# A four-stage transformer block on one core: the two norm chains of a half interleaved, and the ends of the second attention rearranged

## The chip, the cores and the metric

The kernel runs on 1 core of one Trainium2 chip, all in fp32. The metric is the device time of one execution in microseconds (us). Before the change it was 1282.84, 1287.16 and 1286.2 us in three runs, a median of 1286.2 us.

A core has a matrix engine (TensorE, PE in the profile, with its weight loads shown apart as PEld), a vector engine (VectorE, DVE), an activation engine (ScalarE, ACT), a general engine (GpSimd, POOL) and a queue that issues transfers (SyncE, SP). Each works through its own instructions in order and waits for others by semaphores.

## The reference

The input is x, 1024 tokens of 256 channels. Four blocks follow each other, each added to x by the same rule:

```python
x = x + _layernorm(attn0(_layernorm(x)))   # softmax attention, 16 heads of 16, rope, own norm and residual inside
x = x + _layernorm(ffn0(_layernorm(x)))    # 8 experts of 256, all used, low-rank terms in two, routed weights
x = x + _layernorm(attn1(_layernorm(x)))   # 16 heads of 128: short convolution, silu, norm, then the recurrence
x = x + _layernorm(ffn1(_layernorm(x)))    # 16 experts of 176, top 4 of them weighted, and a shared one of 352
```

The recurrence of the second attention, for each head, is `S = (1 - b) * S + b * (v outer k)` and `o = S q`; o is multiplied by a silu gate and goes through Wo. Thus between any two blocks stand two layer norms: one of the block's output (added to x), and one of the new x (input of the next block).

## The kernel before

The kernel is written for a framework that allots tiles from pools and whose scheduler places each instruction in its engine's queue; calls marked to stay in program order keep their order. Tokens lie in 8 tiles of 128 (TT), worked in two halves of 512, a half in two pairs of tiles. Names that recur: `x` and `acc` hold the residual and the block's output by token; `hT` holds the normed x by channel, the input of the next block's matmuls.

*The two norms between blocks.* `turn_over` (L248) takes a pair when its `acc` is complete. For each tile DVE takes statistics (`st`, `mv`), forms `ve`; POOL raises it to −0.5 (`rs`); DVE forms `nb`, minus mean times rs. Then x becomes acc·rs + x (L257), the same statistics are taken of the new x, ACT writes h = x·rs2 + nb2 (L263), POOL adds the first norm's nb to x (L267), and PE transposes h (`turn`, L243), ACT copying to `hT` (L244). The mean of the first norm is left out of x at first, since the second norm takes it away; the POOL operation puts it in afterwards. The transposes are put on a list `todo`, which `catch_up` works off between later matmuls. `turn_over_slowly` (L194) is the same as a generator, advanced in steps beside the first attention; its lines are L201 to L236.

*First attention.* For two halves of queries and four groups of heads (8 steps), scores are computed twice: once to find each row's maximum (L517 and L448 scores, DVE reduces at L453), which goes into the query as an additional channel (`signed`, whose transposes are at L406 and copy at L407), and once transposed, exponentiated by ACT (L546, L535) and summed with the values by PE (L504). The two run interleaved; when no more maxima are left, the last group runs alone (`alone`). In the second half `finished_slowly` (L553) finishes the first half's tokens step by step; the second half's go on `todo` as `finished(1)`, with the product with `w_out` (L601) and its addition (L605).

*Experts.* A group of tiles of 128 hidden columns is worked by halves: `gates` calls `gated` (L757; pg, pu at L765, silu L767, product `mid` L768), then `catch_up`; `down` (L770 on; po L783, acc L791) projects back. `experts` (L795) orders them. In the last group's second half it runs two gate tiles, the previous half's down, the other tiles, and then the last down, calling `turn_over` for each pair.

*Second attention.* Heads run in pairs (groups g). `enter` makes keys and queries through `convolved` (px L1049, taps L1035 and L1041, silu L1059), beta through `shares` (pb L1007), decays (L1012), values and gates (L1183). `attend` does the recurrence in chunks of 128: transposed keys `ke` (L1225), scores `psc`/`pr` (L1231, L1233), states (L1239 to L1248), output `po` and `og` (L1257 to L1265). For the last head `output` projects head 14's and head 15's share by halves, so that `turn_over` can begin; at the end four of the norm chains run one after the other.

## Time and profile before

| what | us |
|---|---|
| median of three runs | 1286.2 |
| the profiled execution's time | 1286.36 |
| its span, first to last instruction | 1284.6 |
| PE busy | 1217.4 |
| DVE busy | 732.4 |
| ACT busy | 495.7 |
| POOL busy | 149.3 |
| mean granted clock of PE | 0.986 |

The first attention ends at about 304 us, the first experts at 488, the second attention at 1004, the second experts with the span. A row of the windows gives a stretch (from:to), its length, each engine's busy time with the number of its instructions, PE's granted clock (1.00 is full), the DMA share and GB/s. A row of the timeline gives the start, the length in us, the engine, the source line, what is written from what, how many instructions are taken together, and in brackets the engine's idle time before and what ended it.

### The profile page before, as it was taken

Reading aid. Unit: us, or ns where it says so; the run is one execution under the profiler, and the core shown is the slowest. Engines: PE = TensorE matmul, PEld = TensorE weight load, DVE = VectorE, ACT = ScalarE, POOL = GpSimd, SP = SyncE. Lnnn points to the kernel's source line nnn. Section 1 sums busy time; section 2 is a strip of 40 time slices with the busy share of each in tenths; the row PEclk is TensorE's granted clock in tenths of the full one; section 3 lists DMA queues with packets and bytes.
Section 4 is the critical chain, followed back from the end, with each engine's and each line's share of the span. In section 5 each row is a group of like instructions: output and inputs, shape, how many; then the busy total and the mean of one; then the engine's idle time right before and its main releaser. Section 6 shows DMA issues by size and latency. Waiting matters only on the chain. (4 is left out here: it accounts for less than half of the span.)

```text
span 1284.6 us, 15784 instructions
## 1 busy us (share of the span) xinstructions
PE 1217.4 (95%) x6128; PEld 722.3 (56%) x6128; DVE 732.4 (57%) x1656; ACT 495.7 (39%) x912; POOL 149.3 (12%) x137
## 2 busy tenths in 40 slices
PE   7999999989999997899999999999998799999997
PEld 4533333323556564567676667767676346555655
DVE  5876767641542345776777776758675523333334
ACT  4266665655411113544544454453543221111011
POOL 3100001010200022121111112121212400000001
PEclk9999999999999998999999999999999899999999
DMA  6000000000033012002021202020210105523000
GB/s 194 1 1 1 1 1 1 1 1 1 2 129 102 0 42 83 29 33 88 23 103 34 74 33 74 34 74 33 74 41 27 62 1 158 163 82 124 20 25 33
DMA packets 38923, 64.42 MB, mean 50 GB/s; under 512 B 4776, under 2 KB 28552, under 8 KB 38848
## 3 DMA queue, kind: packets, MB, share of 16 engines
q1 hardware_dynamic: 38848, 63.41, 15.4%
q8 instruction: 48, 0.79, 0.3%
q14 instruction: 27, 0.22, 0.1%
HBM read 62.12 MB, written 1.28 MB: 49 GB/s over the span
## 5 line engine op out<-in xcount | busy, mean ns | idle before, releaser
L453 DVE TENSOR_REDUCE pm<-sc 128x1 f32<-128x512 f32 x256 | 163.4, 685 | 66.1 <-PE sc L517 42.9
L768 DVE TENSOR_TENSOR mid<-sg,pu 128x512 f32<-128x512 f32 (+1 forms) x82 | 56.4, 688 | 192.7 <-PE pu L765 163.4
L517 PE MATMUL sc<-qTm,kT 32*128 32x512 f32 x512 | 152.5, 654 | 1.2 <-DVE pm L453 1.2
L767 ACT ACTIVATE sg<-pg 128x512 f32<-128x512 f32 (+1 forms) x82 | 48.9, 596 | 270.5 <-PE pg L765 270.4
L546 ACT ACTIVATE pe<-sc 128x512 f32<-128x512 f32 x216 | 117.8, 595 | 71.0 <-PE sc L517 48.8
L448 PE MATMUL sc<-kT,qT 32*128 32x512 f32 x512 | 139.1, 645 | 1.6 <-ACT qT L407 0.8
L1089 ACT ACTIVATE sn<-pt,shift,rs 128x128 f32<-128x128 f32 x256 | 93.6, 470 | 107.2 <-DVE shift L1085 107.0
L1049 PE MATMUL px<-hT,w_l1a 128*128 128x512 f32 x256 | 124.0, 596 | 4.3 <-issue 3.5
L1041 DVE SCALAR_TENSOR_TENSOR y<-px,cp,y 128x1023 f32<-128x1023 f32 (+5 forms) x102 | 123.2, 1211 | 2.5 <-ACT y L1035 2.5
L791 DVE TENSOR_TENSOR acc<-acc,po 128x512 f32<-128x512 f32 (+1 forms) x61 | 41.1, 674 | 100.1 <-PE po L783 100.1
L765 PE MATMUL pg<-hT,w_l1f 128*128 128x512 f32 (+1 forms) x200 | 97.1, 609 | 0.7 <-ACT hT L244 0.7
L765 PE MATMUL pu<-hT,w_l1f 128*128 128x512 f32 (+1 forms) x200 | 94.7, 596 | 0.0
L783 PE MATMUL po<-w_l1f,mid 128*128 128x256 f32 (+1 forms) x400 | 87.5, 379 | 0.0
L1084 POOL TENSOR_TENSOR rs<-ve,nhalf 128x8 f32<-128x8 f32 x32 | 52.4, 1638 | 299.8 <-DVE ve L1083 245.1
L504 PE MATMUL po<-pe,va 128*32 128x256 f32 (+1 forms) x872 | 80.9, 440 | 4.0 <-ACT oT L509 3.3
L783 PEld LDWEIGHTS po<-w_l1f,mid 128*128 128x128 f32 (+1 forms) x400 | 76.0, 190 | 13.4 <-issue 3.3
L517 PEld LDWEIGHTS sc<-qTm,kT 32*128 32x128 f32 x512 | 49.7, 187 | 53.7 <-issue 41.9
L184 POOL TENSOR_TENSOR rs<-ve,nhalf 128x2 f32<-128x2 f32 (+1 forms) x25 | 17.5, 701 | 464.2 <-DVE ve L183 459.7
L1183 PE MATMUL pg<-hT,w_l1a 128*128 128x512 f32 x128 | 61.9, 609 | 6.9 <-DVE og L1265 5.5
L504 PEld LDWEIGHTS po<-pe,va 128*32 128x32 f32 x872 | 17.8, 108 | 89.0 <-issue 77.5
L765 PEld LDWEIGHTS pu<-hT,w_l1f 128*128 128x128 f32 (+1 forms) x200 | 38.5, 192 | 49.5 <-issue 49.5
L765 PEld LDWEIGHTS pg<-hT,w_l1f 128*128 128x128 f32 (+1 forms) x200 | 38.1, 192 | 44.9 <-issue 43.5
(205 smaller groups left out, 1932.6 us busy)
## 6 DMA issues: line engine op xcount, KB each, us to landing
spread<-rows SPq DMA_DIRECT2D x32, 512.0 KB, 4.5
w<-w SPq DMA_DIRECT2D x16, 512.0 KB, 4.9
w_l1f<-in_e_gT SPq DMA_DIRECT2D x4, 640.0 KB, 4.0
w_l1f<-in_e_uT SPq DMA_DIRECT2D x4, 640.0 KB, 5.3
w_l1f<-in_e_dT SPq DMA_DIRECT2D x4, 640.0 KB, 8.0
w_l0f<-in_e_wg SPq DMA_DIRECT2D x4, 512.0 KB, 5.0
w_l0f<-in_e_wu SPq DMA_DIRECT2D x4, 512.0 KB, 6.5
w_l0f<-in_e_wd SPq DMA_DIRECT2D x4, 512.0 KB, 7.4
```

The source lines that it names most:

```text
L448: nc.tensor.matmul(sc, raw[r, tt * P : (tt + 1) * P], kT[r, g, half(kh)], start=True, stop=True,)
L453: nc.vector.tensor_reduce(pm[:, tt, 2 * pair + i, kh : kh + 1], sc, AX.X, ALU.max)
L504: nc.tensor.matmul(po[0][rows(j), c], va[:, st, g * G + j, :], pe[j // 2][:, j % 2, c], start=(st == 0), stop=(st == TT - 1 and c.stop == ...
L517: nc.tensor.matmul(sc, kT[rows(j), g, st * P : (st + 1) * P], qm[rows(j), :], start=True, stop=True,)
L546: nc.scalar.activation(pe[pair][:, i, :], sc, AF.Exp, scale=scale)
L765: nc.tensor.matmul(p, w(k), self.hT[:, k, c], start=(k == 0), stop=(k == KC - 1))
L768: nc.vector.tensor_tensor(mid, sg, pu, ALU.mult)
L783: nc.tensor.matmul(po[:, i, :], left[:, at * P : (at + 1) * P], right, start=(n == 0), stop=(n == len(pieces) - 1),)
L1041: nc.vector.scalar_tensor_tensor(y[:, at:hi], px[:, at - j : hi - j], column(cw + 4 * h + 3 - j), y[:, at:hi], ALU.mult, ALU.add,)
L1049: nc.tensor.matmul(px[:, c], w[:, k, hh * DK : (hh + 1) * DK], self.hT[:, k, c], start=(k == 0), stop=(k == KC - 1),)
L1089: nc.scalar.activation(sn[:, n, :], pts[n // 4][:, n % 4, :], AF.Identity, scale=rs[:, n : n + 1], bias=shift[:, n : n + 1],)
L1183: nc.tensor.matmul(pg, wg[:, k, hh * DK : (hh + 1) * DK], self.hT[:, k, c], start=(k == 0), stop=(k == KC - 1),)
```

## The change

- The two generators become one, `turning`, in 12 pieces, and its DVE instructions are pinned in program order. Means and rs of the first norm are kept for all three inner boundaries (`mvs`, `rss`); the first norm's `nb` and the shift of x on POOL at each boundary are gone. `nb` of the second norm is a piece of its own, after a yield.
- `turn_over` runs the first pair up to piece 5 and keeps it; with the second pair it goes on in turns: first to 10, second to 5, first to 12, second to 12.
- `shifted` adds the sum of the three kept shifts to x once, in the second experts at g == 3: four small POOL operations and eight on ACT.
- First attention: once the maxima are finished, `signed` is put off by two steps (`late`), and the finishing generator is advanced twice in each step.
- Experts: in the last group one gate tile, not two, comes ahead of the previous half's down. In the second experts the very first half's gates are done in two parts of 256 columns, with `catch_up(3)` between.
- Second attention, start: `decays` goes by halves, `begin` is cleared on POOL, and for head 0 decays(0), two calls of values and the first gate come before `catch_up`. End: for the last head `attend` is by_token(0), by_token(1), within(0), gathered(0), within(1), then the down of half 0 for both heads, gathered(1), and the half 1 products of both heads summed in two PSUM tiles (`sums`).
- The pools of all four stages get `reuse_waits="tile"`: a new tile waits for the tiles whose space it takes, not for a whole closed pool.

The diff, cut:

```diff
...
@@ -76,6 +76,9 @@
         self.nhalf = self.const.tile([P, TT], F32, name="nhalf")
         nc.gpsimd.memset(self.nhalf, -0.5)
         self.mv0 = self.const.tile([P, TT, 2], F32, name="mv0")
+        self.mvs = self.const.tile([P, 3, TT, 2], F32, name="mvs")
+        self.rss = self.const.tile([P, 3, TT], F32, name="rss")
+        self.norms = [0] * (TT // 2)
...
-        with tc.tile_pool(name="late", bufs=1) as late:
+        with tc.tile_pool(name="late", reuse_waits="tile", bufs=1) as late:
...
-        nc = self.nc
+    def pinned(self, ins):
+        return self.tc.keep_in_program_order(ins)
+    def turning(self, ps, tp, acc=None):
+        nc, pinned = self.nc, self.pinned
         xs, accs = self.pair(self.x, tp), self.pair(self.acc, tp)
         def small(tag, *shape):
@@ -198,41 +207,48 @@
         def stats(mv, i, src):
             st = self.small.tile([P, 6], F32, tag="st", name="st")
-            nc.vector.bn_stats(st, src)
-            nc.vector.bn_aggr(mv[:, i, :], st)
-        def scale(mv):
-            ve, rs, nb = small("ve"), small("rs"), small("nb")
-            nc.vector.tensor_scalar(ve, mv[:, :, 1], EPS, None, ALU.add)
+            pinned(nc.vector.bn_stats(st, src))
+            pinned(nc.vector.bn_aggr(mv[:, i, :], st))
+        def scale(mv, rs):
+            ve = small("ve")
+            pinned(nc.vector.tensor_scalar(ve, mv[:, :, 1], EPS, None, ALU.add))
             nc.gpsimd.tensor_tensor(rs, ve, self.nhalf[:, 0:2], ALU.pow)
-            nc.vector.scalar_tensor_tensor(nb, mv[:, :, 0], -1.0, rs, ALU.mult, ALU.mult)
-            return rs, nb
-        mv = small("mv", 2)
+        n = self.norms[tp]
+        self.norms[tp] += 1
+        mv, rs = (v[:, n, 2 * tp : 2 * tp + 2] for v in (self.mvs, self.rss))
         for i in range(2):
-            acc(i)
+            if acc is not None:
+                acc(i)
             yield
             stats(mv, i, accs[i])
             yield
-        rs, nb = scale(mv)
+        scale(mv, rs)
         yield
-        mv = small("mv", 2)
+        mv2, rs2 = small("mv", 2), small("rs")
         for i, x in enumerate(xs):
-            nc.vector.scalar_tensor_tensor(x, accs[i], rs[:, i : i + 1], x, ALU.mult, ALU.add)
+            pinned(nc.vector.scalar_tensor_tensor(x, accs[i], rs[:, i : i + 1], x, ALU.mult, ALU.add))
             yield
-            stats(mv, i, x)
+            stats(mv2, i, x)
             yield
-        rs2, nb2 = scale(mv)
+        scale(mv2, rs2)
+        yield
+        nb = small("nb")
+        pinned(nc.vector.scalar_tensor_tensor(nb, mv2[:, :, 0], -1.0, rs2, ALU.mult, ALU.mult))
+        yield
         h = self.row.tile([P, 2, D], F32, tag="h2", name="h")
         for i, x in enumerate(xs):
             nc.scalar.activation(
-                h[:, i, :], x, AF.Identity, scale=rs2[:, i : i + 1], bias=nb2[:, i : i + 1]
+                h[:, i, :], x, AF.Identity, scale=rs2[:, i : i + 1], bias=nb[:, i : i + 1]
             )
-            yield
-        for i, x in enumerate(xs):
-            nc.gpsimd.tensor_scalar(x, x, nb[:, i : i + 1], None, ALU.add)
+        ps = (yield) or ps
         self.turn(ps, h, tp)
         yield
+    SCALED, NORMED, PIECES = 5, 10, 12
...
-        xs = self.pair(self.x, tp)
-        rs, nb = self.scales(self.pair(self.acc, tp))
-        for i, x in enumerate(xs):
-            nc.vector.scalar_tensor_tensor(
-                x, self.acc[:, 2 * tp + i, :], rs[:, i : i + 1], x, ALU.mult, ALU.add
-            )
-        rs2, nb2 = self.scales(xs)
-        h = self.row.tile([P, 2, D], F32, tag="h2", name="h")
-        for i, x in enumerate(xs):
-            nc.scalar.activation(
-                h[:, i, :], x, AF.Identity, scale=rs2[:, i : i + 1], bias=nb2[:, i : i + 1]
-            )
-        for i, x in enumerate(xs):
-            nc.gpsimd.tensor_scalar(x, x, nb[:, i : i + 1], None, ALU.add)
-        self.todo.extend([None, None, lambda ps: self.turn(ps, h, tp)])
+        def take(t, n):
+            for _ in range(n):
+                next(t)
+        t = self.turning(ps, tts[0] // 2)
+        if tts[0] // 2 % 2 == 0:
+            take(t, self.SCALED)
+            self.first_pair = t
+            return
+        first = self.first_pair
+        take(first, self.NORMED - self.SCALED)
+        take(t, self.SCALED)
+        take(first, self.PIECES - self.NORMED)
+        take(t, self.PIECES - self.SCALED)
+        for t in (first, t):
+            self.todo.extend([None, None, lambda ps, t=t: t.send(ps)])
+    def shifted(self):
+        nc = self.nc
+        lost = self.small.tile([P, 3, TT], F32, tag="lost", bufs=1, name="lost")
+        shift = self.small.tile([P, TT], F32, tag="shift", bufs=1, name="shift")
+        nc.gpsimd.tensor_tensor(lost, self.mvs[:, :, :, 0], self.rss, ALU.mult)
+        nc.gpsimd.tensor_tensor(shift, lost[:, 0, :], lost[:, 1, :], ALU.add)
+        nc.gpsimd.tensor_tensor(shift, shift, lost[:, 2, :], ALU.add)
+        nc.gpsimd.tensor_scalar(shift, shift, -1.0, None, ALU.mult)
+        for tt in range(TT):
+            x = self.x[:, tt, :]
+            self.pinned(nc.scalar.activation(x, x, AF.Identity, bias=shift[:, tt : tt + 1]))
...
-            after = iter(())
+            after, then, late = iter(()), None, 2
             for n, (qh, g) in enumerate(steps):
                 if n == NG:
                     after = finished_slowly()
-                then = None
                 for inside in attend(qh, g, lambda: pulled == count):
                     if inside:
                         then = pull()
                         continue
-                    if then:
+                    if pulled == count and late > 0:
+                        late -= 1
+                    elif then:
                         then()
                         then = None
                     next(after, None)
+                    if pulled == count:
+                        next(after, None)
...
+    def gated(self, ps, tmp, wg, wu, mid, m, hf, part=None):
+        nc = self.nc
+        part = part or slice(0, HALF)
+        n = part.stop - part.start
+        c = slice(hf * HALF + part.start, hf * HALF + part.stop)
+        mid = mid[:, part]
+        pg = ps.tile([m, n], F32, tag="b1", name="pg")
+        pu = ps.tile([m, n], F32, tag="b1", name="pu")
...
+            if join and (g, hf) == (0, 0):
+                for part in (slice(0, HALF // 2), slice(HALF // 2, HALF)):
+                    for i, (wg, wu, right, m, row) in enumerate(tiles):
+                        self.gated(ps, tmp, wg, wu, mid[0:m, i, :], m, hf, part)
+                    if part.start == 0:
+                        self.catch_up(ps, 3)
+                return
             for i, (wg, wu, right, m, row) in list(enumerate(tiles))[some]:
...
+            if join and g == 3:
+                self.shifted()
...
-                    gates(half, slice(0, 2))
+                    gates(half, slice(0, 1))
                     down(behind.pop(0))
-                    gates(half, slice(2, None))
+                    gates(half, slice(1, None))
                     self.catch_up(ps, len(self.todo))
                     down(half)
...
+            nc.gpsimd.memset(begin, 0.0)
+            def decays(hf):
+                n = slice(hf * NC // 2, (hf + 1) * NC // 2)
+                pt = ps.tile([P, NC // 2, H], F32, tag="b1", name="pt")
+                for i in range(NC // 2):
+                    nc.tensor.transpose(pt[:, i, :], beta[:, hf * NC // 2 + i, :], self.ident[0:H, 0:H])
+                nc.scalar.copy(btok[:, n, :], pt)
+                nc.vector.tensor_scalar(decay[:, n, :], beta[:, n, :], -1.0, 1.0, ALU.mult, ALU.add)
+                nc.vector.tensor_copy(begin[:, n, 0:1], decay[:, n, 0:1])
+                nc.vector.memset(decay[:, n, 0:1], 0.0)
+                nc.vector.tensor_tensor_scan(
+                    flat(prod[:, n, :]), flat(decay[:, n, :]), flat(begin[:, n, :]), 0.0,
+                    ALU.mult, ALU.add,
+                )
+                if hf == 1:
+                    nc.sync.dma_start(out=rows[0], in_=flat(decay))
+                    nc.sync.dma_start(out=rows[1], in_=flat(prod))
...
+                next(k_)
+                if h == 0:
+                    shares(0)
+                    next(q_)
+                    decays(0)
+                    next(v_)
+                    next(v_)
+                    gated(0)
+                    self.catch_up(ps, len(self.todo))
+                    shares(1)
+                    decays(1)
+                for i in range(2):
+                    nc.sync.dma_start(out=spread[:, i, :], in_=rows[i, h, :].partition_broadcast(P))
+                next(k_)
+                yield
+                if h > 0:
+                    next(v_, None)
+                    next(v_, None)
+                yield
+                if h > 0:
+                    next(q_)
+                next(q_)
+                next(k_)
+                yield
+                next(v_, None)
+                next(v_, None)
+                nc.vector.tensor_tensor_scan(
+                    dec.rearrange("p c t -> p (c t)"), spread[:, 0, :],
+                    idr.rearrange("p c t -> p (c t)"), 0.0, ALU.mult, ALU.add,
+                )
+                yield
+                next(k_)
+                next(q_)
+                yield
+                for hf in range(2):
+                    if (h, hf) != (0, 0):
+                        gated(hf)
                 yield
...
+                wo = groups[g][4]
+                if h == H - 1:
+                    by_token(0)
+                    by_token(1)
+                    within(0)
+                    gathered(0)
+                    within(1)
+                    c = slice(0, HALF)
+                    self.down(
+                        ps, [(og[:, i, c], wo[:, i, :]) for i in range(HG)], False, 0, self.turn_over
+                    )
+                    gathered(1)
+                    sums = [ps2.tile([P, 2, HALF], F32, tag="x2", name="sums") for _ in range(2)]
+                    for i in range(HG):
+                        for tt in range(TT // 2, TT):
+                            at = tt - TT // 2
+                            nc.tensor.matmul(
+                                sums[at // 2][:, at % 2, 0:D], og[:, i, tt * P : (tt + 1) * P],
+                                wo[:, i, :], start=(i == 0), stop=(i == HG - 1),
+                            )
+                    for tp, po in zip(range(TT // 4, TT // 2), sums):
+                        dst = self.acc[:, 2 * tp : 2 * tp + 2, :]
+                        nc.vector.tensor_tensor(dst, dst, po[:, :, 0:D], ALU.add)
+                        self.turn_over(ps, [2 * tp, 2 * tp + 1])
+                    self.catch_up(ps, 3)
+                    self.load_next()
+                    return
...
```

## The prediction

> **What bounds the kernel now.** I read the page's busy times first, then the granted clock, then the windows and the timeline around each place that the diff touches.
>
> ```profile
> PE 1217.4 (95%) x6128; PEld 722.3 (56%) x6128; DVE 732.4 (57%) x1656; ACT 495.7 (39%) x912; POOL 149.3 (12%) x137
> PEclk9999999999999998999999999999999899999999
> ```
>
> TensorE (PE) is busy for 1217.4 of 1284.6 us. The change issues 12 more matmul instructions on PE with the same columns in all, so PE's work stays. There are two things to win: PE's idle time, 1284.6 − 1217.4 = 67 us, of which only the part at the touched places counts, and the stretches in which the granted clock is halved. The windows show those:
>
> ```profile
> core 0: us, PE busy (x) PEld busy (x) DVE busy (x) ACT busy (x) POOL busy (x), PEclk, DMA share, GB/s
> 215.50:218.60 3.10, 3.09 (x24) 0.76 (x16) 2.96 (x8) 0.63 (x2) 0.05 (x1) 1.00 0.00 0
> 218.60:222.00 3.40, 2.19 (x16) 1.03 (x14) 2.54 (x7) 1.99 (x5) 1.99 (x3) 1.00 0.00 0
> 222.00:228.80 6.80, 6.80 (x29) 2.59 (x26) 3.13 (x5) 3.21 (x7) 0.54 (x1) 0.50 0.00 0
> ...
> 478.00:481.40 3.40, 1.68 (x9) 1.34 (x10) 1.46 (x3) 2.15 (x4) 2.42 (x3) 1.00 0.00 0
> 495.10:498.50 3.40, 0.29 (x3) 0.06 (x1) 2.89 (x9) 0.93 (x3) 0.73 (x1) 1.00 0.00 0
> 498.50:505.30 6.80, 5.75 (x13) 1.99 (x14) 0.23 (x1) 2.08 (x4) 1.84 (x2) 0.50 0.00 0
> 1003.70:1007.10 3.40, 0.00 (x0) 0.00 (x0) 3.18 (x10) 0.00 (x0) 1.04 (x2) 1.00 1.02 402
> 1007.10:1013.90 6.80, 4.98 (x9) 2.30 (x10) 3.89 (x19) 1.91 (x4) 3.58 (x6) 0.50 0.22 72
> ```
>
> The column after POOL is the granted clock. It reads 0.50 for 6.80 us at 222, 498.5 and 1007 (and at 283.5), each time after a stretch in which PE lacked work. At 0.50 a full PE does half its work, so each costs up to 3.4 us beside the gap that went before. The first comes from this:
>
> ```profile
> 215.58 0.16 DVE L208 SCALAR_TENSOR_TENSOR nb<-mv,rs 128x2 f32<-128x2 f32 x1 [0.82 <-POOL rs L207]
> ...
> 219.81 0.16 DVE L208 SCALAR_TENSOR_TENSOR nb<-mv,rs 128x2 f32<-128x2 f32 x1 [0.81 <-POOL rs L207]
> 219.89 2.48 DVE L453 TENSOR_REDUCE pm<-sc 128x1 f32<-128x512 f32 x4
> 220.01 1.09 ACT L228 ACTIVATE h<-x,nb,rs 128x256 f32<-128x256 f32 x2 [3.27 <-DVE nb L208]
> 220.63 0.29 PEld L517 LDWEIGHTS sc<-qTm,kT 32*128 32x128 f32 x2 [1.69 <-DVE pm L453]
> 220.63 1.12 PE L517 MATMUL sc<-qTm,kT 32*128 32x512 f32 x2 [1.21 <-DVE pm L453]
> ```
>
> Twice VectorE (DVE) stands 0.8 us at nb until GpSimd (POOL) has rs; the row maxima L453 queue behind it, and PE waits 1.21 us for a free score bank.
>
> **1. Middle of the first attention (213–229).** After, the chain is cut into 12 pieces pinned in program order; nb is a piece of its own, two steps after rs is asked for, so rs (0.71) is there when nb comes, and between two pieces the maxima go on. DVE still has the chain's other work (about 0.45 for each stats or x), but DVE was busy 12.94 of 17.00 us here, so it fits. nb of the first norm (0.16) is gone. The gap of 1.21 goes. What of the half clock? The Trainium skill (TensorE: Matmul & The Clock Gate, "What's actually happening") has the clock halved after at least one idle window of about 3.4 us. By that rule 218.6–222 (PE 2.19 busy of 3.40) is no idle window, the drop is not due to this chain, and the sum here is −1.2. The rows say otherwise: directly after that stretch the clock is halved, though after 478–481.4, with less PE busy (1.68), it isn't. The stretch that dropped held matmuls that use 32 rows only, the other full ones; I take the row: the gap causes the drop, so −1.2 − 3.4 = **−4.6** (ends −1.2 and −4.6, and +2 if the pieces delay other maxima).
>
> **2. End of the first attention (270–305).** Signed (the copy qTm and its transposes) is put off two steps, and the other norm pieces come twice as fast. PE's 1.06 gap before qTm's transposes at 271.70 is filled by a step. In ACT's order, however, h of the last pair now stands before four exponentials, and nb comes near 281, so ACT waits there about 3.3 (2.07 before, the row at 283.69). These cancel to within my reading. What is left: pair 1's h (0.60), its turn (0.66) and copy hT (0.59) no longer stand last before the experts' gates, of which about 1.3 shows at 301–305: **−1.3** (−3 to +1; the half clock at 283.5 stays).
>
> **3. First gates of experts0 (322–335).** PE has no gap here before. After, the fourth w_out product and its acc (L605, 0.48) stand behind a tile's gates in PE's order, and pair 2's nb stands behind mid (0.69) on DVE, which is pinned behind it. PE comes to pair 2's turn with this left: 0.3 rest of mid's wait + 0.69 mid + 0.4 stats + 0.6 h (ACT) + 0.15 = **+2.1** (0 to +3; nothing if the tile ahead is long enough to cover it).
>
> **4. End of experts0 and start of the second attention (456–545).**
>
> ```profile
> 479.67 0.93 PE L243 MATMUL pt<-ident,h 128*128 128x128 f32 x4 [2.47 <-ACT h L263]
> ...
> 489.27 1.96 PE L1049 MATMUL px<-hT,w_l1a 128*128 128x512 f32 x4 [1.76 <-issue]
> ...
> 498.88 1.18 PE L243 MATMUL pt<-ident,h 128*128 128x128 f32 x4 [3.48 <-ACT h L263]
> ```
>
> down(half 0) of the last group starts one gate tile (3.43 us) earlier; the interleaved chains then leave PE about 0.2 + 1.2 of waiting instead of 2.47, and the last down starts about 1.0 earlier. px waited 1.76 although nothing in the row is late: it is the first PSUM tile of a new pool, and the acc add at 488.52 + 0.65 = 489.17 is the last reader of the old one. With reuse by tile it waits for one old tile: −1.76. Values, decays(0) and gated(0), some 5.3 us of PE work, move into the hole before 498.88. But the chain that follows isn't shortened: pair 3's nb shares DVE with decay, scan and vb, and ACT, in order, must do a table load (1.28 at 493.19 before), the gate 0.6, hT of pair 2 and hT of pair 3 (0.6 each), so hT(3) is there at about 502.5 (500.68 before), then reloads for beta(1): two loads more, 2 × 1.28. (The skill, ScalarE: Activation LUTs, "What ACT_TABLE_LOAD costs", gives 1.28 for the load but 2.66 with its drain; the rows here show 1.28 from 493.19 to the next start at 494.49, so 1.30; by the page this chain would be 2.7 later.) PE then idles from about 498 to 502.5 and the half clock comes again. Head 0's silu k is at 512.4–515.6 (512.35 before), and what PE had gained early it waits for at psc. Of 2.76 I keep **−0.5** (−3 to +2). begin's memset (0.91) goes from DVE to POOL, hidden behind PE; the rows' two DMAs still go after the second half, so spread is as late as beta(1).
>
> **5. End of the second attention (984–1014).**
>
> ```profile
> 1001.73 0.93 POOL L267 TENSOR_SCALAR x<-x,nb 128x256 f32<-128x256 f32 x1 [0.93 <-ACT h L263]
> 1002.63 0.73 POOL L184 TENSOR_TENSOR rs<-ve,nhalf 128x2 f32<-128x2 f32 x1
> ...
> 1008.25 1.18 PE L243 MATMUL pt<-ident,h 128*128 128x128 f32 x4 [5.63 <-ACT h L263]
> ...
> 1010.10 1.22 PE L765 MATMUL pg<-hT,w_l1f 128*128 128x512 f32 x1 [0.68 <-ACT hT L244]
> ```
>
> Pair 1's rs queues 0.9 behind the shift of x on POOL, its chain runs behind pair 0's, and PE stands 5.63 us. After: ke and pr come before the acc adds, og of half 0 at 989.95 (992.00); down 991.5–995.05, acc 993.3 and 995.1; gathered(1) to 997.4; og 997.6; the sums to 1000.1, two issued early; the adds of 0.69 to acc are 4 here, not 8. Pair 0's nb at 1002.1, h to 1003.25, hT 1004.2: the first gates, on 256 columns, start at 1004.25 instead of 1010.10. They are 5.2 us of work. Then the second columns need hT of pair 1, whose h ends at 1007.9; but in ACT's order h of pair 2 stands between, and its nb comes at about 1011.8 (acc add 1000.5, rs behind pair 1's, two mids of 0.45 on DVE). So 1011.85 + 1.1 + 0.6: hT(1) at 1013.55, and PE goes on at 1013.6 with 5.2 done, whether the clock was half in between or not. Before, at 1013.88, one pg of two matmuls, 1.72, was done. 5.2 − 1.72 + 0.28 = **−3.75** (−1 to −7: a second clock drop after the stall, or none at all). The weights are no cover: group 0's were issued at 961, group 1's go at 1000.1 instead of 1001.63.
>
> **6. Rest of experts1: 0.** 24 shifts of 0.93 us, 22 us of POOL, are gone, POOL being 12% busy; only the one above was on the path. For them come 4 small POOL operations, queued ahead of pair 3's rs (up to 2.8 us; hT of pair 3 has over 5 us of gates for cover), and 8 ACT operations of about 0.55 (the h row: 1.09 for two), 4.4 us, while ACT is busy 35 of 240 us from 1040 on and PE 237. Without that cover they would cost 4.4.
>
> **Sum.** −4.6 − 1.3 + 2.1 − 0.5 − 3.75 = −8.05. The profiled execution took 1286.36 us around a span of 1284.6; the median shown is 1286.2. 1286.2 − 8.05 = 1278.15; I say **1278**.
>
> **Rivals.** A change under 0.3% (3.9 us) can't be told from none.
> - *The drop at 222 stays or moves* (the skill's rule is right, or another window in this stretch of 32-row matmuls gets too short): 1278.2 + 3.4 = **1281.6**. For it: the idle share alone doesn't sort the rows above. Against: PE is full from 215.5 to 218.6 and from 222.
> - *More drops go* (283.5 or 1007, filled by pieces 2 and 5): one or two times 3.4, **1271 to 1275**. Against: PE still idles for 4 us in both.
> - *In-order waits take the place of those removed*: hT behind the next pair's h, beta behind two table loads, mid ahead of nb; steps 3, 4 and 5 at their bad ends are +3 + 2 − 1: with −4.6 and −1.3 it is −1.9, **1284**, no change.
> - *Slower*: the pieces, now spread from 213 to 270, hold a maximum late in window after window, PE idles about a microsecond in each, and the clock drops again and again where it dropped once. Each drop costs 3.4 and its gap 1.2: from three on the gain of 8 is gone (13.8 − 8), and the time is **1292**. For it: one gap of 1.21 sufficed at 219.42. Against: DVE has 4 of 17 us free here.
>
> **How the numbers follow.** Mine 0.50 (1274.5 to 1282), drop stays 0.18, more drops go 0.15, in-order waits 0.10, slower 0.07. Faster by over 0.3%, that is under 1282.3: 0.48 + 0.12 + 0.15 = 0.75; slower 0.07; the rest, 0.18, is the same. A tenth at each end gives the range: 1271.5 below (into the third case), 1286 above (past the fourth).
>
> **What would show it.** Right: no 0.5 in PEclk at 222–229, no PE gap of over 1 us there; no x<-x,nb on POOL; a new gap of about 2 us at pair 2's turn near 330; px right behind the last down; the first experts1 gates some 6 us earlier relative to the last qn, followed by a gap of 1 to 3.5 us before the second columns, ended by hT. Wrong: half clock between 213 and 270 in any place; gates of the first experts without a gap (step 3 too dear); silu k of head 0 over 3 us late (step 4 too cheap).

## The result and the profile after

The changed kernel took 1279.85 us (median of 6 runs, 1274.77 to 1280.06), the kernel before, run beside it, 1285.19 us (1282.84 to 1287.16). The ratio is 0.9944, with a 95% interval of 0.993 to 0.9957. A second set of six gave 1278.77 us (1278.26 to 1279.64) against 1285.76; all twelve of the changed kernel together have a median of 1279.2, which is what the experiments below are compared with. The forecast was 1278.

The profiled execution of the changed kernel is its fastest, 1274.77 us with a span of 1272.7; so it is 4.4 us below that median, and for the sums below the second profile of the same kernel, of an execution of 1278.26 us, stands beside it. The page of the first, busy times and granted clock:

```profile
PE 1214.0 (95%) x6152; PEld 727.1 (57%) x6152; DVE 732.0 (58%) x1646; ACT 501.0 (39%) x926; POOL 127.8 (10%) x118
PEclk9999999999899999999999999999999999999999
```

PE is busy 3.4 us less than before (1217.4; 1217.7 in the second profile), and POOL has lost 21.5 us. The clock row's two eights have become one, in another slice; the second profile has three, so this row alone doesn't tell the kernels apart. The windows of the places that the prediction named (from:to, length, busy time of PE, PEld, DVE, ACT and POOL with the number of instructions, granted clock, DMA share, GB/s):

```profile
218.60:222.00 3.40, 3.40 (x24) 0.76 (x18) 2.39 (x5) 2.03 (x4) 0.71 (x1) 1.00 0.00 0
222.00:228.80 6.80, 6.80 (x68) 2.49 (x64) 5.85 (x11) 4.34 (x8) 0.00 (x0) 1.00 0.01 2
274.60:278.00 3.40, 1.12 (x2) 0.29 (x2) 0.11 (x1) 3.25 (x7) 0.00 (x0) 1.00 0.00 0
278.00:281.40 3.40, 3.10 (x16) 0.72 (x16) 0.00 (x0) 2.21 (x5) 0.00 (x0) 0.50 0.00 0
322.40:325.80 3.40, 1.42 (x6) 0.59 (x5) 2.51 (x11) 1.09 (x2) 1.39 (x2) 1.00 0.00 0
325.80:329.20 3.40, 3.40 (x6) 1.33 (x5) 1.99 (x8) 0.98 (x2) 0.70 (x1) 0.50 0.00 0
503.30:506.70 3.40, 0.00 (x0) 0.00 (x0) 3.40 (x5) 1.71 (x3) 0.00 (x0) 1.00 0.09 14
506.70:513.50 6.80, 5.88 (x14) 3.65 (x15) 4.76 (x5) 1.83 (x2) 0.00 (x0) 0.50 0.92 309
994.80:998.20 3.40, 1.29 (x6) 0.80 (x7) 2.48 (x10) 1.68 (x3) 0.69 (x1) 1.00 0.96 323
998.20:1001.60 3.40, 3.40 (x10) 2.66 (x9) 1.90 (x11) 1.47 (x3) 1.39 (x2) 0.50 0.75 259
```

At 218.6 to 228.8 PE is full at full clock: the gap of 1.21 us and the halved clock are gone. At the other ends PE still idles and the clock still halves, and there is a new pair at 322 to 329, where the kernel before had none.

To see where the time went, the execution is cut at marks that all kernels share, each the start of the named instruction in the trace (for the last down and the last matmul: its end). Lengths in us, in brackets the start of a halved-clock window that falls in the piece, with its length:

| piece | before | after, 1274.8 | after, 1278.3 |
|---|---|---|---|
| start to first gates of experts0 | 304.76 (222: 6.8; 283.5: 6.8) | 296.40 (278: 3.4) | 297.59 (277.7: 6.8) |
| to the end of their last down | 182.75 | 186.51 (325.8: 3.4; 339.4: 3.4) | 185.33 (339.2: 3.4) |
| to the first px | 1.76 | −0.17 | −0.16 |
| to head 0's first psc | 48.20 (498.5: 6.8) | 49.36 (506.7: 6.8) | 50.85 (499.6: 3.4; 506.4: 6.8) |
| to head 14's first psc | 426.28 | 426.69 | 426.51 |
| to the first gates of experts1 | 46.35 (1007.1, in part) | 38.99 | 39.25 (997.9, in part) |
| to their first down | 63.93 (1007.1, rest; 1044.6: 3.4) | 64.27 (998.2: 3.4) | 66.35 (997.9, rest; 1035.5: 3.4) |
| to the last matmul | 203.26 | 203.38 | 203.26 |
| sum | 1277.29 | 1265.43 | 1268.98 |

Against before, the second execution gains 7.2 in the first attention and 7.1 at the second attention's end, 1.9 at px, and gives 2.6 back in the first experts, 2.7 at the second attention's start and 2.4 after the last experts' first gates: 16.2 won, 7.7 given back, with 0.2 in the middle. Nearly half of what was won is given back. And 1.3 of the 7.2 is chance: PE's wait before the first scores ends at 27.05 us before and at 25.77 in this execution, but anywhere from 25.4 to 27.4 in the profiles of the experiments below, most of which don't differ there.

The two profiles of one kernel differ by 3.55 us. They do so in four pieces, each where the halved windows differ: +1.19 (6.8 instead of 3.4 at 278), −1.18 (no window at 326), +1.49 (one more at 499.6), +2.08 (6.8 instead of 3.4 at 998, and one at 1035.5). A window of 3.4 us at half clock costs a full PE 1.7 us.

### The profile page after: what moved, and what is told of

It is laid out like the page before. It is cut to its first block, busy times and chain, and to the rows that moved or that the text cites. A ratio compares the mean times of both kernels' runs of the same rounds, so it can differ in the third digit from the quotient of the medians.

```text
span 1272.7 us, 15799 instructions
## 1 busy us (share of the span) xinstructions
PE 1214.0 (95%) x6152; PEld 727.1 (57%) x6152; DVE 732.0 (58%) x1646; ACT 501.0 (39%) x926; POOL 127.8 (10%) x118
## 5 line engine op out<-in xcount | busy, mean ns | idle before, releaser
L806 DVE TENSOR_TENSOR mid<-sg,pu 128x512 f32<-128x512 f32 (+2 forms) x85 | 56.7, 667 | 194.1 <-PE pu L803 190.7
L805 ACT ACTIVATE sg<-pg 128x512 f32<-128x512 f32 (+2 forms) x85 | 49.4, 581 | 280.9 <-PE pg L803 280.9
L476 PE MATMUL sc<-kT,qT 32*128 32x512 f32 x512 | 136.3, 638 | 1.6 <-ACT qT L435 0.8
L803 PE MATMUL pg<-hT,w_l1f 128*128 128x512 f32 (+3 forms) x212 | 95.7, 574 | 2.1 <-ACT hT L260 2.1
L803 PE MATMUL pu<-hT,w_l1f 128*128 128x512 f32 (+3 forms) x212 | 95.4, 573 | 0.0
L829 DVE TENSOR_TENSOR acc<-acc,po 128x512 f32<-128x512 f32 (+1 forms) x55 | 37.2, 676 | 94.0 <-PE po L821 94.0
L803 PE MATMUL pg<-hT,w_l0f 128*128 128x512 f32 x128 | 62.8, 612 | 0.0
```

What stands on the lines that cost most here:

```text
L476: nc.tensor.matmul(sc, raw[r, tt * P : (tt + 1) * P], kT[r, g, half(kh)], start=True, stop=True,)
L803: nc.tensor.matmul(p, w(k), self.hT[:, k, c], start=(k == 0), stop=(k == KC - 1))
L806: nc.vector.tensor_tensor(mid, sg, pu, ALU.mult)
```

## The experiments

Each is the changed kernel with one thing altered; where an edit has two parts, both are named. The last starts from the version that is uninterleaved at the second attention's end. Executions of one kernel lie 1 to 8 us apart, so differences of medians under about 1.5 us decide nothing; then the pieces of the trace do.

**The same kernel again.** No edit.

> The changed kernel once more, nothing altered. Its six times fell into two groups, 1274.8 to 1275.9 and 1279.7 to 1280.1. Theory: the groups are due to the clock gate, whose halved windows fall differently from execution to execution; then a new profile shows the same rows in the same order with other places at 0.5, and any two executions differ by multiples of about 1.7 to 3.4 us. Rival: a wait on a transfer or semaphore that comes out in two ways; then the profiles differ in a gap at one place while the clock rows are alike. Both: median 1275 to 1280.

Measured 1278.77 us. The windows of its profile:

```profile
277.70:284.50 6.80, 6.29 (x28) 1.44 (x32) 0.00 (x0) 4.48 (x9) 0.00 (x0) 0.50 0.00 0
335.80:339.20 3.40, 3.40 (x27) 3.01 (x27) 0.73 (x3) 0.26 (x1) 0.00 (x0) 0.99 0.01 2
339.20:342.60 3.40, 3.40 (x5) 1.35 (x4) 1.27 (x6) 1.21 (x1) 0.00 (x0) 0.50 0.00 0
1035.50:1038.90 3.40, 3.40 (x7) 1.73 (x7) 2.42 (x15) 0.31 (x1) 0.00 (x0) 0.50 0.02 5
```

PE's gaps of over 1 us are the same in both profiles within 0.05 us, but one (1.45 or 0.89 us before the second columns); the halved windows are others. The theory holds for these two executions: the clock gate makes their difference. The row at 335.8 is worth a look. PE counts as busy for all of it, with the 32 small router matmuls (128x8 outputs, 3.63 us from 334.85), and the clock halves right after. Whether a window of the gate happens to lie over such a burst differs from execution to execution.

**First attention: the chain not pinned.**

```diff
-        nc, pinned = self.nc, self.pinned
+        nc = self.nc
+        pinned = self.pinned if acc is None else (lambda ins: ins)
```

> The changed kernel, but the finishing chain beside the first attention is not pinned on DVE (the experts' chains still are). Theory of step 1 (pinning spreads the chain and so removes the gap and the halved clock at 222): the chain is lumped again, a gap of about 1.2 us ended by the maxima returns near 219, the clock halves after it, and the first experts' gates start 4 to 5 us later than with the change (296.4 to about 301); time +4.6, about 1284. Rival (the split of nb, not the order, did it): start of the gates within 1 us of 296.4, time as the changed kernel.

Measured 1282.85 us (22 runs, 1278.69 to 1286.55), +3.7 against 1279.2. The timeline of its profile, and one window:

```profile
218.06 0.16 DVE L240 SCALAR_TENSOR_TENSOR nb<-mv,rs 128x2 f32<-128x2 f32 x1 [0.81 <-POOL rs L217]
218.13 2.48 DVE L482 TENSOR_REDUCE pm<-sc 128x1 f32<-128x512 f32 x4
218.87 1.63 PE L546 MATMUL sc<-qTm,kT 32*128 32x512 f32 x2 [1.21 <-DVE pm L482]
```

```profile
219.40:222.80 3.40, 3.40 (x14) 2.79 (x14) 2.43 (x5) 2.70 (x6) 0.00 (x0) 0.50 0.00 0
```

The gap is back to the hundredth, 1.21, and so is the halved clock, here for one window. In this execution (1279.89, near the fastest of its 22) the first gates come at 298.17, not at 301 as expected. Counted from PE's first wait for scores, which ended at 25.37 here and at 25.88 in the first profile of the changed kernel, that is 2.3 later than in that profile, with a halved stretch of 3.4 us near 280 in both. So the rows show the mechanism, and the median the size of 3.7; the rival, that the split of nb did it, fails.

**First attention: nb directly after rs.**

```diff
         scale(mv2, rs2)
-        yield
+        if acc is None:
+            yield
```

> The changed kernel, but beside the first attention nb follows directly on rs (no step between), pinned as it is. Theory of step 1 (the 0.8 us in which DVE stands at nb is what makes PE's gap): a DVE wait of 0.8 at nb near 235 to 250 returns and with it a PE gap of about 1 us and, by the row at 222, a halved clock: gates 1 to 4.6 us later, time 1281 to 1284. Rival (with the pieces spread, one wait of 0.8 is absorbed by the score banks): no gap, gates within 0.5 us of 296.4, time unchanged.

Measured 1278.22 us, −1.0: no difference that can be told. DVE does stand:

```profile
240.10 0.16 DVE L240 SCALAR_TENSOR_TENSOR nb<-mv,rs 128x2 f32<-128x2 f32 x1 [0.81 <-POOL rs L216]
```

but PE has no gap of 0.6 us or more between 42.66 and 274, the clock isn't halved before 337, and the gates come at 296.05. The one gap over 0.5 in this stretch, 0.57 at 241.92, ends with ACT's pe, which stood behind h, and not with a maximum. The rival holds: the wait of 0.8 is absorbed, once the pieces are spread.

**Whole pools instead of tiles.** The argument `reuse_waits="tile"` removed everywhere.

> The changed kernel with the stage pools waiting for whole pools again. Theory of step 4 (px waited for the last reader of the old pool): the gap of about 1.8 us before the first px returns, and the first gates of the last experts wait for the last reader of the second attention's pool as well, which now runs late: those gates, at 997.8 in the changed kernel, start 3 to 6 us later; time +3 to +7. Rival (the waits are covered by norm chains): only px is later, which the chain at 503 absorbs, time within 1.5 us of the changed kernel.

Measured 1279.52 us, +0.3. Px waits 0.83 us after the last down, not 1.76; the last experts' first gates are no later (997.38), but the second columns wait 3.14 instead of 0.9 to 1.5, and from the first gates to the first down it is 68.77 us instead of 66.35. The rival was right on the time of six runs. That the waits are covered was not shown: this profile has no halved window in the first experts, which makes up for the loss at the end.

**The chains one after the other, at all three boundaries.**

```diff
-        if tts[0] // 2 % 2 == 0:
-            take(t, self.SCALED)
-            self.first_pair = t
-            return
-        ...
+        take(t, self.PIECES)
+        self.todo.extend([None, None, lambda ps: t.send(ps)])
```

> The changed kernel with the two chains of a half one after the other again (each pair's 12 pieces in one go), still pinned, nb still a piece. Theory of steps 3 to 5: the interleave costs at the first experts' start (pair 2's nb stands behind pair 3's pieces and mid), so the gap of 1.98 us near 324 shrinks to about 0.5 to 1, and it pays at the two other ends: the last down of the first experts starts about 1 us later, the first gates of the last experts are equal (pair 0 comes first either way), their second columns wait about 2 us longer. Net +1 to +2.5 us, about 1280.5. Rival (pinning in a fixed order does it all): no gap differs by more than 0.3 us, time unchanged.

Measured 1275.26 us (1272.92 to 1277.92), −3.9: neither expectation. PE's longest wait at the first experts' start:

```profile
332.95 0.44 PE L259 MATMUL pt<-ident,h 128*128 128x128 f32 x2 [3.35 <-ACT h L243]
```

At the first experts' start the waits grow to 0.90 + 3.35 us (1.98 when interleaved), contrary to the theory. Yet the whole piece, 184.83 us, is no longer than the changed kernel's 185.33 and 186.51, which have one and two halved windows where this one has none. An interleaved piece without any is the one with whole pools, 183.64; by that comparison of two profiles the interleave pays about 1.2 us here. At the end of the second attention it costs, contrary to both: 38.16 us from head 14's first score to the first gates (39.25), and 63.50 to the first down (66.35).

**The same at the second attention's end alone.**

```diff
         t = self.turning(ps, tts[0] // 2)
+        if self.norms[tts[0] // 2] == 2:
+            take(t, self.PIECES)
+            self.todo.extend([None, None, lambda ps: t.send(ps)])
+            return
```

> The changed kernel with the chains of a half one after the other only at the end of the second attention (its third use); at the experts they stay interleaved. With all three undone the time fell to 1275.3. Theory A (the interleave costs at the end: pair 0's nb and h wait about 1 us behind pair 1's statistics, hT of pair 1 behind h of pair 2, and the longer idle of PE halves the clock at 998): the gap before pair 0's turn is 1.6 instead of 2.4, the one before the second columns 0.7 instead of 0.9 to 1.5, no or less half clock at 995 to 1005, from the first gates to the first down product 61.5 to 63.5 us instead of 64.3 to 67.7; time -3 against the changed kernel, about 1275.5. Theory B (the gain came from the first experts, whose half-clock windows at 326 to 339 were absent): that stretch 66 us and the time within 1 us of the changed kernel, 1278 to 1280.

Measured 1274.18 us (1270.61 to 1275.62), −5.0; its ratio to before is 0.9916 (0.9904 to 0.9929), better than the changed kernel's. Theory A holds. The timeline of the changed kernel at this place, then of this one:

```profile
993.77 0.70 POOL L216 TENSOR_TENSOR rs<-ve,nhalf 128x2 f32<-128x2 f32 x1 [3.31 <-DVE ve L215]
993.93 0.67 DVE L1351 TENSOR_TENSOR acc<-acc,sums 128x512 f32<-128x512 f32 x1
...
995.33 0.15 DVE L239 SCALAR_TENSOR_TENSOR nb<-mv,rs 128x2 f32<-128x2 f32 x1
995.52 1.09 ACT L243 ACTIVATE h<-x,nb,rs 128x256 f32<-128x256 f32 x2 [15.75 <-DVE nb L239]
996.18 0.93 PE L259 MATMUL pt<-ident,h 128*128 128x128 f32 x4 [2.43 <-ACT h L243]
997.78 1.26 PE L803 MATMUL pg<-hT,w_l1f 128*128 128x256 f32 x3 [0.67 <-ACT hT L260]
...
1005.19 1.09 ACT L243 ACTIVATE h<-x,nb,rs 128x256 f32<-128x256 f32 x2 [0.72 <-DVE nb L239]
1006.19 0.56 ACT L260 COPY hT<-pt 128x512 f32<-128x512 f32 x1
1006.80 0.48 PE L803 MATMUL pg<-hT,w_l1f 128*128 128x256 f32 x1 [1.45 <-ACT hT L260]
```

```profile
993.18 0.70 POOL L216 TENSOR_TENSOR rs<-ve,nhalf 128x2 f32<-128x2 f32 x1 [3.31 <-DVE ve L215]
993.91 0.16 DVE L239 SCALAR_TENSOR_TENSOR nb<-mv,rs 128x2 f32<-128x2 f32 x1 [0.41 <-POOL rs L216]
993.99 0.68 DVE L1355 TENSOR_TENSOR acc<-acc,sums 128x512 f32<-128x512 f32 x1
994.76 0.93 PE L259 MATMUL pt<-ident,h 128*128 128x128 f32 x4 [1.60 <-ACT h L243]
...
1002.92 1.13 PE L807 MATMUL pg<-hT,w_l1f 128*128 128x256 f32 x4 [0.67 <-ACT hT L260]
```

In the changed kernel rs of pair 0 is there at 994.47 (993.77 + 0.70), but nb runs at 995.33: the last acc add and pair 1's statistics stand ahead of it, the statistics pinned. Uninterleaved, nb runs as soon as rs is there, and PE's idle falls from 2.43 to 1.60. Then the clock, in this kernel's windows:

```profile
991.10:994.50 3.40, 1.99 (x8) 1.44 (x8) 2.95 (x12) 0.40 (x1) 0.70 (x1) 1.00 0.12 13
994.50:997.90 3.40, 2.41 (x11) 1.78 (x12) 2.45 (x9) 1.65 (x4) 0.70 (x1) 1.00 0.95 352
997.90:1001.30 3.40, 3.40 (x18) 2.80 (x17) 2.21 (x11) 1.61 (x5) 1.39 (x2) 1.00 0.65 218
```

No window is empty enough, and none is halved. Nor is this one lucky execution: all ten profiles with interleaved chains at this place have a halved window that starts between 995 and 1006; the three without (the one before, this one and the last one below) have none there. From the first gates to the first down it is 61.80 us, against 64.27 and 66.35 with the change. Before the first gates 0.83 us of idle time went, before the second columns 0.2 to 0.8; with the clock they became 2.5 to 4.6 us after the first gates.

**The old order of the last head.** Early projection of head 14's half 0, both halves' states before any output, eight adds into acc; new norm chains. The edit also turns both pairs before the gates (`catch_up(6)`).

> The changed kernel with the second attention's last head in its old order (head 14's half 0 projected early, states of both halves before any output, eight adds into acc), new norm chains kept. Theory of step 5 (the early down and the sums let the chains start some 2 us earlier; the rest of the 7 us comes from the chains themselves and from the columns): the stretch from head 14's first score to the first gates, 46.35 before and 39.0 to 39.3 with the change, becomes 41 to 43; time +2 to +4. Rival (the new order did all of it): 46, time +7; rival (nothing): 39, time +0.

Measured 1280.7 us, +1.5, PE's turns:

```profile
999.55 1.01 PE L259 MATMUL pt<-ident,h 128*128 128x128 f32 x4 [3.89 <-ACT h L243]
1004.19 1.18 PE L259 MATMUL pt<-ident,h 128*128 128x128 f32 x4 [3.63 <-ACT h L243]
```

The stretch to the first gates is 45.46 us, nearly the 46.35 of before, as the first rival had it. But both pairs are turned ahead of the gates here, which saves a wait after them: to the first down the two stretches are 108.43 together, 105.60 with the change (second profile), 2.8 more, and the time follows that rather than the 7 us. The next experiment turns both pairs first as well, with the new order, and takes 107.94 on the same stretch with one halved window more. So what the order alone is worth lies between 0.5 and 2.8 us and isn't settled; the earlier start of the gates overstates it.

**Whole columns at the last experts' first gates.** The `join and (g, hf) == (0, 0)` block removed, `catch_up(6)` before.

> The changed kernel, but the last experts' first gates take all 512 columns at once, after both pairs are turned. Theory of step 5 (half-width gates give PE 5.2 us of work while pair 1's chain runs): the first gates start 5 to 7 us later and the stretch from head 14's first score to the first down product is 2 to 3.5 us longer than with the change (105.6 in its like execution); time +2 to +3.5. Rival (PE waits for pair 1 anyway, and the half clock of a longer wait is all): +0 to +1.

Measured 1279.08 us, −0.1. PE waits twice before the gates:

```profile
997.44 1.18 PE L259 MATMUL pt<-ident,h 128*128 128x128 f32 x4 [2.43 <-ACT h L243]
1002.08 1.18 PE L259 MATMUL pt<-ident,h 128*128 128x128 f32 x4 [3.46 <-ACT h L243]
```

The stretch from head 14's first score to the first down is 107.94 us, 2.3 more than 105.60, as the theory had it, but the median shows none of it. With six runs each and windows that move, 2.3 us in one profile is not settled; what can be said is that the split gates are worth no more than about 2 us.

**Head 0's first gate left where it was.**

```diff
                     next(v_)
                     next(v_)
-                    gated(0)
```

> The changed kernel, but head 0's first gate is not pulled ahead of the norm chains (both gates where they were); so ACT has no table load for silu and no reload for sigmoid between the first and second beta. Theory of step 4 (the order on ACT, hT of pair 3 behind a load of 1.28 and the gate of 0.60, then a reload of 1.28, ate the lead): hT of pair 3 and beta(1) 2 to 3 us earlier, the gap of 5.14 us before px at 504 falls to about 2 to 3; from the first px to the first psc 48 us where the changed kernel takes 49.4 to 51; time -2 to -3, about 1276. Rival (the taps on DVE set it): that stretch the same within 0.5 us, as PE has the gate's 1.9 us to do later; time +0 to +1.

Measured 1277.82 us, −1.4. Up to head 0's first psc it is 47.52 us, 3.3 less than 50.85, as the theory had it, but up to head 14's it is 429.39, 2.9 more than 426.51. The rival has the time: what was gained is lost later, partly in a wait of 1.80 us before px at 534.92. That the gate, done later, is the reason was not tested.

**The end of the first attention as it was.** `late = 0`, and one piece of the chain per step.

> The changed kernel without the two edits at the end of the first attention: signed is not put off, the finishing generator goes one piece per step. Theory of step 2 as the traces now show it (faster pieces take pair 1's turn and hT out of the end, and the wait of 3.3 us at 281 becomes 1.9 + 0.8): the first experts' gates, 296.4 to 297.6 with the change, come at 299 to 301, with a gap of about 3 us near 280 and halved clock for two windows; time +2.5 to +3.5. Rival of step 2 (the waits cancel, only 1.3 us at 300 counts): gates at 298, time +1.3.

Measured 1280.66 us, +1.5. In its profile the clock isn't halved near 280, and the first gates come at 296.59; the first profile of the changed kernel is at 296.40 with a halved window, in which PE was busy 3.10 us and so lost 1.55. Without it, it would be at 294.85. So the two edits are worth about 1.7 us where the clock is alike; nearer the rival's 1.3 than 2.5 to 3.5.

**The shift of x put back at each boundary.** First norm's nb on DVE beside the second's, two POOL additions after h, no `shifted`.

> The changed kernel with the shift of x put back at each boundary (first norm's nb on DVE without a wait, two POOL additions of 0.93 after each h), and no shift on ACT in the last experts. Theory of step 6 and 5 (only where rs queues behind the additions at the ends is it on the path): pair 1's rs near 999 and pair 2's near 1003 start up to 1 us later each, the second columns' gap grows by 1 to 2 us; elsewhere nothing; time +1 to +2.5. Rival (the 8 ACT additions cost as much as is saved, or the queue is free when rs comes): time within 0.7 us.

Measured 1280.46 us, +1.3. The two additions together hold POOL for 2.1 to 2.3 us at each pair, but rs waits for its own ve there, not for the queue; the gap before the second columns is 1.43 us, inside what the changed kernel shows itself. Its profile has more time at half clock than the changed kernel's first one at 500, 998 and 1036. The difference is not settled; no wait behind the additions explains it.

**Beta in a buffer of its own, with the chains uninterleaved at the end.** The one experiment on what the prediction hadn't seen. The changed kernel's longest gap is the one that leads to the windows at 503 to 513 above, in its timeline:

```profile
502.17 1.45 ACT L1090 ACTIVATE y<-px,cp 128x512 f32<-128x512 f32 x2 [1.24 <-PE px L1104]
502.99 1.42 DVE L1096 SCALAR_TENSOR_TENSOR y<-px,cp,y 128x512 f32<-128x512 f32 x2 [1.29 <-ACT y L1090]
...
505.45 2.68 DVE L1096 SCALAR_TENSOR_TENSOR y<-px,cp,y 128x510 f32<-128x510 f32 x4
507.62 1.19 PE L1104 MATMUL px<-hT,w_l1a 128*128 128x512 f32 x1 [5.14 <-DVE y L1096]
```

The second half of the first query's px waits for the taps of its first half, whose input was there at 488.36. Their y has tag y with two buffers: one has the key, the other beta.

```diff
-            beta, decay, begin, prod = (
-                two.tile([H, NC, C], F32, tag=t, name=s)
-                for t, s in (("y", "beta"), ("qg", "decay"), ("sn", "begin"), ("gate", "prod"))
+            beta = one.tile([H, NC, C], F32, name="beta")
+            decay, begin, prod = (
+                two.tile([H, NC, C], F32, tag=t, name=s)
+                for t, s in (("qg", "decay"), ("sn", "begin"), ("gate", "prod"))
```

> The kernel with the chains uninterleaved only at the second attention's end, and beta in a buffer of its own instead of one of the two of tag y. Theory (the gap of 5.14 us before the last px of head 0 comes from y of the first query, which needs the buffer that beta holds until the second decays have read it; its first taps, and the second half of px behind them, can't start before 503): with the buffer free, those taps run before 496, the gap falls below 2.5 us, from the first px to the first psc 46 to 48 us instead of 49.1 to 51, and the time is 1 to 3 us less, 1271.5 to 1273. Rival (beta(1), the taps of the key and the scans set the pace, as moving the gate showed, where 3.3 us gained up to the first psc came back as waits up to the next heads): the gap goes but head 14's first score is as late as before, time unchanged at 1274.

Measured 1271.02 us (1268.91 to 1276.23), ratio to before 0.9899 (0.9881 to 0.9917). ACT and PE in its timeline:

```profile
488.47 0.76 ACT L1095 ACTIVATE y<-px,cp 128x512 f32<-128x512 f32 x1
```

```profile
508.06 4.51 PE L1109 MATMUL px<-hT,w_l1a 128*128 128x512 f32 x6 [2.56 <-DVE y L1101]
```

The taps run at 488 and the gap falls to 2.56 us: the cause of the 5.14 is shown. The stretch to head 0's first psc, 50.52, doesn't get shorter as expected (49.10 without the buffer), which was the rival's sign; from there to head 14's it is 424.45, 2.1 less. The time is 3.2 below the uninterleaved kernel's, but the ranges of the two overlap (1270.61 to 1275.62 there), so how much the buffer brings isn't settled. It is the best version run, 14 us under the kernel before.

## Why the prediction was right or wrong

The direction and the size were right (−8.05 forecast, −5.3 and −7.0 in the two sets), but the size partly by luck: step 3's piece cost 1.5 more than the sum had it, step 5's gained 0.9 more, and the profiled execution owes 1.3 to its start. The pieces below are those of the second profile against before.

- *Step 1, −4.6: measured 3.7, and right in one of its two reasons.* Unpinned, the time is 3.7 longer and the gap and the drop are back. The split of nb, which the step named as well, isn't needed: with nb directly behind rs no drop returns and the time is the same. It is the pinned order, which keeps the scheduler from pulling the chain's pieces together ahead of the maxima. Between the row and the rule of the Trainium skill (TensorE: Matmul & The Clock Gate, "What's actually happening") the row was the better guide: a stretch with PE busy 2.19 of 3.40 us was followed by the halved clock twice, in the kernel before and in the unpinned one. Why 1.68 at 478 was not, the last section shows.
- *Step 2, −1.3: about 1.7.* The first attention's piece gained 7.2, of which 1.3 is the chance at its start. The rest is 5.9, the sum of steps 1 and 2. The gap of 1.06 is filled and no wait for hT stands before the gates, as said; ACT's wait for nb is 2.42 us at 274.75, not 3.3 near 281.
- *Step 3, +2.1: measured 1.98*, the gap at pair 2's turn, ended by h:

```profile
322.92 0.69 POOL L216 TENSOR_TENSOR rs<-ve,nhalf 128x2 f32<-128x2 f32 x1 [4.72 <-DVE ve L215]
...
323.61 0.67 DVE L806 TENSOR_TENSOR mid<-sg,pu 128x512 f32<-128x512 f32 x1
...
324.48 0.15 DVE L239 SCALAR_TENSOR_TENSOR nb<-mv,rs 128x2 f32<-128x2 f32 x1
...
325.33 0.44 PE L259 MATMUL pt<-ident,h 128*128 128x128 f32 x2 [1.98 <-ACT h L243]
```

  rs is done at 323.61 and nb runs 0.87 later, behind mid and pair 3's pieces, as said. What the step left out is half clock. The first profile has windows at 326 and 339 here, the second one at 339, each worth 1.7. With the 1.0 won at the last down the forecast for the piece was +1.1; it is +2.6. The window at 339 follows the router's matmuls, which the kernel before has too and where it escaped, so this 1.7 is the place of the windows rather than the change.
- *Step 4, −0.5 net.* Px without its wait: −1.9 (−1.76 said). The stretch after it: +2.7 (+2.3 said). In the first profile, with as much half clock as before, the latter is +1.2, so about half of the 2.7 is clock. The step saw ACT's order and two more table loads; without them 3.3 us were won up to the first psc and 2.9 lost later. It did not see the longest idle, which came from beta holding a buffer, with taps that could have run 14 us earlier; but with a buffer of its own for beta the stretch is no shorter either, so the cause of the rest stays open. The idle was put at 498 to 502.5; it is 2.4 before pb and 5.1 after it. And the −1.76 for reuse by tile does not show in the time: with whole pools px waits 0.83, and the median is the same.
- *Step 5, −3.75: −4.7 (−7.1 and +2.4).* The first gates 7 us earlier, hT of pair 1 behind h of pair 2, and the gap of 0.9 to 1.45 before the second columns were as said. Missed was the interleave's own price here. The step has no term for what stands between rs and nb of pair 0; nb comes 0.86 after rs, and this lengthens an idle stretch that halves the clock. Taking the interleave out at this one place is worth 5.0 us by the medians.
- *Step 6, 0: consistent.* The last piece is 203.26 in both, so 8 additions on ACT are hidden. That shifts on POOL cost 1.0 on the path was not shown.

Of the rivals, "in-order waits" took part, in what was given back at the first experts and the second attention's start, and "more drops go" did in the fastest execution: its halved stretches near 280 and 998 last 3.4 us where the kernel before had 6.8. "Drop stays at 222" is refuted by the windows, and the repeated drops of "slower" did not come: between 42.3 and 274 us PE has no gap of 0.5 in the changed kernel.

## What to carry to other kernels

Interleaving two dependent chains on an in-order engine can help where PE waits for the second chain (3.35 us uninterleaved against 1.98 at the first experts' start). Where PE is idle until the first chain ends, each piece of the second ahead of it is paid in full (0.86 us at the second attention's end), and more if the longer idle stretch halves the clock. Decide it for each boundary, by which result the idle engine waits for, and not once for all calls. When a wait names an engine that was long free, look also at which tile's buffer the late instruction writes: a small early tile in a large shared tag held back 5 us of work.

## What the runs showed of the hardware

The clock windows are 3.41 us long, and the places of the halved ones shift between executions; the two profiles of one kernel, 3.55 us apart, differ by just these. PE's busy time doesn't decide. It was 1.76 us in a window that was followed by half (995.1, in the kernel with the old end of the first attention) and 1.75 in one that wasn't (993.7, in the one with all chains uninterleaved); it was all of 3.40 us in the router window at 335.8, and half followed.

Counting the columns that PE streams in a window sorts them. Each matmul counts with its output columns, by the part of it that lies in the window; one that uses 32 rows or has 32 output rows counts a quarter, since four of these run side by side (eight score matmuls of 512 columns took 1.14 us at full clock, eight gate matmuls of 512 take 3.44). The 14 traces have 4922 windows at full clock between 30 and 1255 us, and 75 were followed by half. Below 1490 columns all were but one (994 columns, at 272.6 in the kernel with nb directly after rs), from 1495 to 1535 three of six, above that none. A window full of gate matmuls, 0.43 us each, holds about 4060, so the edge lies near 37%, by an estimate from these traces that no other kernel has tested. The router window has 908 columns, the one at 994.8 has 797, and those at 991.1 and 994.5 of the kernel uninterleaved at the end have 2048 and 2150. The stretch at 218.6 before has 1151 and the unpinned one at 216 has 1407, but 478 before has 1599. An idle stretch thus does harm by the columns that a window loses, and a stretch of narrow matmuls does the same harm without any idle.

The clock stays at half for one to three windows (10.2 us at 997.7 in the kernel with whole columns).
